# Reordering the drain of a gather-and-project kernel: residuals, put-by sums, the last gathers and the final test

## The chip, the cores and the metric

The kernel runs on one core of one Trainium2 chip. The metric is the device time of one execution in microseconds; the median of several executions counts. The inputs are `x` (4096 x 512), `adj` (4096 x 4096), `W` (512 x 2048, four heads of 512) and `a`, all fp32; the output is 4096 x 512 fp32.

## The reference, cut to what matters

```python
ht  = (h @ W).reshape(N, 4, 512).transpose(1, 0, 2)
src = einsum('hnd,hd->hn', ht, a[:, :512, 0]); dst = einsum('hnd,hd->hn', ht, a[:, 512:, 0])
e   = leaky_relu(src[:, :, None] + dst[:, None, :], 0.01) + adj[None]
att = softmax(e, axis=-1)
x   = layernorm(x + einsum('hij,hjd->hid', att, ht).mean(axis=0))
```

The entries of `adj` reach 1e9, so that in nearly every row one neighbour, the one with the row's largest entry, takes the whole softmax. Then the attention of a row is `x[column of that entry] @ mean over heads of W`. The kernel computes this, and proves it row by row with a bound: the gap between the largest and the second largest entry must exceed a multiple of the largest norm of a row of `x` times the norms of the head vectors. If a row fails, a general path runs behind a branch; with these inputs it does not.

## The kernel before, in words

The 4096 rows stand in 32 blocks of 128 rows (`NB = 32`; a row of a block is a partition). The program is written in the order in which its instructions are to stand; each engine (PE, DVE, ACT, POOL, SP) then runs its own instructions in that order, and one that waits holds back all that stand behind it on its engine.

One pass `t` of the main loop handles a stage of several blocks at once:

- SP loads block `t + 5` of `adj` (2 MB a block, `load_adj`). `hold` holds `x` and later the output rows.
- DVE takes maxima over segments of block `t` (`segment_maxima`, L169), then `find_segment(t)` finds the eight largest (L176) and the best segment's index (L178). POOL turns the index into a row number (L180) and gathers that segment of each row, the "lead" (L186, 128 rows of 128 bytes); it also computes where the segment starts (L191).
- DVE finds the place within the lead of block `t - 2` (`find_column`, L208), POOL adds the segment's start (L210) and gathers the 128 rows of `x` that the columns name (L196, tile `y`, 256 KB).
- PE turns block `t - 3` (`turn`, four transposes, L223), ACT copies the result to SBUF (L225, `yt`), and PE multiplies it by the mean weight in four steps of 128 rows (`products`, L238; a step is two matmuls in the trace[...]), into a PSUM tile `o`. Pool `o` has four buffers of one bank; `tp` has two, `px` and `pv` one each.
- For blocks 0 to 23 PE adds the residual `x` with an identity matmul (`residual`, L231), and ACT takes sums and squares (`stats`, L260 and L262), POOL the reciprocal root (`rstd`, L265 to L267) and ACT writes the normalised row into `hold` (`finish`, L271).

The last eight blocks are special. `BEHIND = 24` and `LATE = 28`. For blocks 24 to 27 ("put by") ACT copies the product out of PSUM to a spare `adj` buffer (`put_by`, L251), because their `x` has not been loaded yet; it is added later (`add_x`, L254). Blocks 28 and 29 get their residual by matmul (L231) in pass 31. Block 30 gets it by a DVE addition (L521), and block 31 is computed in two column halves with residuals of their own (`residual_in_halves`, L276, and `products_of_half`, L280), so that its two halves can be normalised by two engines. Blocks 27 to 31 use DVE statistics (`moments`: L291 and L295 on DVE, a root on ACT, L297; `factor`, L300; `normalise`, L307). Block 31's column is not found through a lead but in the whole row of `adj` (`find_column_in_row`, L216), so that the last gather of `x` need not wait for another gather.

After the loop comes the drain, an order written out by hand. It also holds the proof: `find_inner` (L202) takes the largest entries within the leads of blocks 24 to 31, `bound` (parts 0 to 3) the largest norm of `x` over all rows through two tiny PE operations (L379, L385), `test` six small DVE operations on all blocks (L394 to L400), `count` a tiny matmul (L404) and `report` three small DVE operations (L408 to L411). The stores of the last blocks stand in SP's queue in a fixed order.

In a few lines, the part of the drain around the change before it:

```python
find_column(NB - 2); add_x(nc.gpsimd, BEHIND); add_x(nc.gpsimd, BEHIND + 1)
find_column_in_row(NB - 1); add_x(nc.gpsimd, BEHIND + 2)
products(LATE, KB - 1, KB); residual_in_halves(NB - 1); turn(NB - 3)
```

Of the kernel before, what the change touches and what calls it, by code (L numbers as in the profile page):

```python
# [9 lines left out]
F32 = mybir.dt.float32  # L10
U32 = mybir.dt.uint32
I32 = mybir.dt.int32
AF = mybir.ActivationFunctionType
OP = mybir.AluOpType
# [6 lines left out]
P = 128  # L21
# [47 lines left out]
def leading_rows(ctx, tc, x, adj, W, a, out, ident, v, n_bad, any_bad):  # L69
# [8 lines left out]
    nc = tc.nc  # L78
# [66 lines left out]
    nc.gpsimd.memset(ones, 1.0)  # L145
    width = once.tile([P, 2], U32, name="width")
    nc.gpsimd.iota(width, pattern=[[E_EARLY - E, 2]], base=E, channel_multiplier=0)
    power = once.tile([P, 2], F32, name="power")
    nc.gpsimd.memset(power, -0.5)
    eps = once.tile([P, 1], F32, name="eps")  # L150
    nc.gpsimd.memset(eps, EPS)
# [22 lines left out]
    def find_segment(ib):  # L174
        seg = seg_of.pop(ib)
        nc.vector.max(out=top[:, ib, :], in_=seg)  # L176
        at = small.tile([P, 8], U32, name="at")
        nc.vector.max_index(at, top[:, ib, :], seg)  # L178
        row = small.tile([P, 1], U32, name="row")
        nc.gpsimd.tensor_tensor(row, at[:, 0:1], first[:, ib : ib + 1], op=OP.add)  # L180
        early = ib < EARLY
        if early:
            lead = lead_pool.tile([P, E_EARLY], F32, name="lead_early", bufs=8)
        else:
            lead = lead_pool.tile([P, E], F32, name="lead")
        nc.gpsimd.indirect_dma_start(  # L186
            out=lead, out_offset=None, in_=adj_segs_early if early else adj_segs,
            in_offset=bass.IndirectOffsetOnAxis(ap=row[:, :1], axis=0),
        )
        start = at_of[ib] = small.tile([P, 1], U32, name="start")  # L190
        nc.gpsimd.tensor_tensor(start, at[:, 0:1], width[:, int(early) : int(early) + 1], op=OP.mult)  # L191
        lead_of[ib] = lead

    def gather_rows(ib, col):
        y = y_t[ib] = y_pool.tile([P, D], F32, name="y")
# [5 lines left out]
    def find_inner(ib):  # L201
        nc.vector.max(out=inner[:, ib, :], in_=lead_of[ib])  # L202

    def find_column(ib):
        if ib < BEHIND:
            find_inner(ib)
        within = small.tile([P, 8], U32, name="within")
        nc.vector.max_index(within, top[:, ib, :], lead_of[ib])  # L208
        col = small.tile([P, 1], U32, name="col")
        nc.gpsimd.tensor_tensor(col, at_of.pop(ib), within[:, 0:1], op=OP.add)  # L210
        gather_rows(ib, col)
# [15 lines left out]
    def residual(ib):  # L227
        start = ib not in o_ps
        if start:
            o_ps[ib] = psum.tile([P, D], F32, name="o")  # L230
        nc.tensor.matmul(o_ps[ib], ident, hold[:, ib, :], start=start, stop=False)  # L231

    def products(ib, lo=0, hi=KB):
        start = ib not in o_ps
        if start:
            o_ps[ib] = psum.tile([P, D], F32, name="o")
        for kb in range(lo, hi):
            nc.tensor.matmul(  # L238
                o_ps[ib], yt_of[ib][:, kb, :], w_sum[:, kb, :],
                start=(start and kb == 0), stop=(kb == KB - 1),  # L240
            )

    def row_norm(ib):
        sq = rows.tile([P, D], F32, name="sq")
        nc.scalar.activation(sq, hold[:, ib, :], AF.Square, accum_out=xx[:, ib : ib + 1])  # L245
# [5 lines left out]
        nc.scalar.copy(o_ps["by"][:, ib - BEHIND, :], o_ps.pop(ib))  # L251

    def add_x(engine, ib):
        engine.tensor_add(hold[:, ib, :], hold[:, ib, :], o_ps["by"][:, ib - BEHIND, :])  # L254
        o_ps[ib] = hold[:, ib, :]

    def stats(ib):
        o, i = o_ps[ib], slice(ib, ib + 1)
# [14 lines left out]
    def residual_in_halves(ib):  # L273
        o_ps[ib] = [psum.tile([P, D // 2], F32, name="o") for _ in range(2)]
        for k, o in enumerate(o_ps[ib]):
            nc.tensor.matmul(o, ident, hold[:, ib, ts(k, D // 2)], start=True, stop=False)  # L276
# [45 lines left out]
    def store(queue, lo, n):  # L322
        queue.dma_start(out_rows[:, ds(lo, n), :], hold[:, ds(lo, n), :])
# [49 lines left out]
    def bound(part):  # L373

        if part == 0:
            xm = once.tile([P, 1], F32, name="xm")
            nc.vector.tensor_reduce(xm, xx, axis=AX.X, op=OP.max)
            px = of_bound[0] = psum.tile([1, P], F32, name="px", bufs=1)
            nc.tensor.transpose(px, xm, ident)  # L379
        elif part == 1:  # L380
            nc.vector.tensor_reduce(xg, of_bound[0], axis=AX.X, op=OP.max)
            nc.scalar.activation(xg, xg, AF.Sqrt)
        elif part == 2:
            pb = of_bound[2] = psum.tile([P, 1], F32, name="px", bufs=1)
            nc.tensor.matmul(pb, ones[0:1, :], xg, start=True, stop=True)  # L385
        else:
            nc.vector.tensor_mul(lead_by, of_bound[2], vn)
            nc.vector.tensor_scalar(lead_by, lead_by, 1.05, 110.0, op0=OP.mult, op1=OP.add)
# [29 lines left out]
    for t in range(NB):  # L418
        if t == NB // 2:
            tc.mark_branch_hint_location("general", engines=HINTED)  # L420
        if t in x_at:
            load_x(*x_at[t])
        if t + AHEAD == NB - 1:
            load_x(LATE, Q)
        load_adj(t + AHEAD)
        middle = 1 if t == NB - 1 else 2
        segment_maxima(t, 0, middle)
        if t >= COLUMN:
            find_column(t - COLUMN)
        segment_maxima(t, middle, PIECES)  # L430
        pair = FINISH <= t < BEHIND + FINISH and t % 2 == 0
        if pair:
            rstd(slice(t - FINISH, t - FINISH + 2))
        if t == NB - 1:
            for ib in (BEHIND, BEHIND + 2):
                load_x(ib, 2)
        find_segment(t)
        if t < 2:
            mean_of_heads(t)
        elif t == 2:  # L440
            mean_of_heads(2)
            mean_of_heads(3)
        if t == 0:
            turn_a()
        turned = [(*vectors[0], turn_w(*vectors.pop(0))) for _ in range(vectors_at.get(t, 0))]
        if t == 16:
            head_norms()
        ib = t - PROJECT
        if t == NB - 1:
            for late in range(LATE, NB):  # L450
                row_norm(late)
            residual(LATE)
            residual(LATE + 1)
        if ib >= 0:
            turn(ib)
            if ib > BEHIND:
                products(ib - 1, KB - 1, KB)
            if ib < BEHIND:
                residual(ib)
        for some in turned:  # L460
            head_vector(*some)
        if ib >= 0:
            products(ib, 0, KB if ib < BEHIND else KB - 1)
        if t >= BEHIND + STATS:
            put_by(t - STATS)
        elif t >= STATS:
            stats(t - STATS)
            row_norm(t - STATS)
        if pair:
            finish(t - FINISH)  # L470
            finish(t - FINISH + 1)

    for ib in range(BEHIND, LATE):
        row_norm(ib)
    for ib in range(0, 2 * Q, Q):
        store(nc.sync, ib, Q)
    for ib in range(2 * Q, BEHIND, 2):
        store(nc.sync, ib, 2)
    find_column(NB - 2)
    add_x(nc.gpsimd, BEHIND)  # L480
    add_x(nc.gpsimd, BEHIND + 1)
    find_column_in_row(NB - 1)
    add_x(nc.gpsimd, BEHIND + 2)
    products(LATE, KB - 1, KB)
    residual_in_halves(NB - 1)
    turn(NB - 3)
    products(NB - 3, 0, KB - 1)
    moments(LATE)
    for ib in range(BEHIND, NB):
        find_inner(ib)  # L490
    bound(0)
    products(NB - 3, KB - 1, KB)
    stats(BEHIND)
    factor(LATE)
    normalise(LATE, o_ps.pop(LATE))
    bound(1)
    turn(NB - 2)
    bound(2)
    add_x(nc.vector, LATE - 1)
    stats(BEHIND + 1)  # L500
    moments(LATE - 1)
    products(NB - 2, 0, 2)
    bound(3)
    test()
    pg = count()
    products(NB - 2, 2, KB - 1)
    stats(BEHIND + 2)
    rstd(slice(BEHIND, BEHIND + 2))
    rstd(slice(BEHIND + 2, BEHIND + 3))
    moments(NB - 3)  # L510
    report(pg)
    turn(NB - 1)
    factor(LATE - 1, shift=True)
    factor(NB - 3)
    normalise(NB - 3, o_ps.pop(NB - 3))
    finish(BEHIND)
    finish(BEHIND + 1)
    products(NB - 2, KB - 1, KB)
    products_of_half(NB - 1, 0)
    products_of_half(NB - 1, 1)  # L520
    nc.vector.tensor_add(hold[:, NB - 2, :], o_ps[NB - 2], hold[:, NB - 2, :])  # L521
    o_ps[NB - 2] = hold[:, NB - 2, :]
    moments(NB - 2)
    stats_of_half(NB - 1, 0)
    factor(NB - 2)
    normalise(NB - 2, o_ps.pop(NB - 2))
    finish(BEHIND + 2)
    finish(BEHIND + 3)
    stats_of_half(NB - 1, 1)
    moments(NB - 1)  # L530
    factor(NB - 1, shift=True)
    finish_in_halves(NB - 1)
    for ib, n in ((NB - 4, 1), (NB - 3, 1), (BEHIND, 2), (NB - 2, 1), (BEHIND + 2, 2)):
        store(nc.sync, ib, n)
    store(nc.sync, NB - 1, 1)

# [152 lines left out]
```

## Time and profile before

| What | Value |
|---|---|
| Median of 3 runs | 236.35 us (236.19 to 236.41) |
| The profiled execution's own time | 235.55 us |
| Its span in the profile | 233.9 us |
| Granted clock of PE over the span | 0.965 |
| PE busy | 197.9 us (85%) |
| DVE busy | 192.0 us (82%) |
| ACT busy | 111.8 us (48%) |
| POOL busy | 101.1 us (43%) |
| DMA | 97.06 MB, mean 415 GB/s |
| Last load of `adj` landed, last PE matmul ended | 207.6 us, 228.64 us |

The span runs from the first to the last instruction of the profiled execution; the execution's own time is 1.65 us longer, for what lies around it. Times below are microseconds from the start of the span. The drain proper is the stretch from 207.6 us to the end: the last quarter of `adj` block 31 is in SBUF, and what remains is the search in the last blocks, the last gathers of `x`, the products of blocks 28 to 31, and the normalisation and stores of blocks 24 to 31. The table's shares of busy time are over the whole span and say little about these 26 us; the timeline and the chain of waits do.

### The profile page before, as it was taken

The numbers are of one execution on the slowest core, as the hardware profiler recorded it, in microseconds if no ns is written. First come the engines' busy times: TensorE is split into PE (matmuls) and PEld (weight loads), VectorE is DVE, ScalarE is ACT, GpSimd is POOL, SyncE is SP. The second block draws the span as 40 slices with busy tenths as digits, with TensorE's granted clock in tenths as the row PEclk, the third lists the DMA queues.
The fourth block names the chain that finished last, engine by engine and source line by source line (L and its number), as shares of the span: only waits on it lengthen the run. The fifth ranks groups of instructions, "written<-read, shape, count | busy, mean of one in ns | idle before, by whom it ended". The sixth has DMA issues, their size and how long they took to land.

```text
span 233.9 us, 2499 instructions
## 1 busy us (share of the span) xinstructions
PE 197.9 (85%) x683; PEld 103.0 (44%) x683; DVE 192.0 (82%) x302; ACT 111.8 (48%) x267; POOL 101.1 (43%) x216
## 2 busy tenths in 40 slices
PE   0097959999999899999969968888886989998990
PEld 0034526565656565655424424343433434334460
DVE  1726975689969996999689999998699999979872
ACT  2002012155756547474747464646464285355782
POOL 2022242415526462646343555464364546438330
PEclk9999799999999999999997999999995899999997
DMA  5999999999999999999999999999999999999995
GB/s 226 443 419 424 443 419 432 430 433 413 438 427 417 425 434 434 432 417 426 432 430 436 421 435 423 433 413 433 426 429 418 424 423 425 418 423 416 418 371 220
DMA packets 13697, 97.06 MB, mean 415 GB/s; under 512 B 2152, under 2 KB 2664, under 8 KB 7792
## 3 DMA queue, kind: packets, MB, share of 16 engines
q1 hardware_dynamic: 10080, 88.08, 89.1%
q0 software_dynamic: 3584, 8.77, 9.5%
q8 instruction: 6, 0.10, 0.2%
q14 instruction: 11, 0.09, 0.1%
q10 hardware_dynamic: 16, 0.02, 0.0%
HBM read 88.47 MB, written 8.39 MB: 414 GB/s over the span
## 4 chain that ended last, share of the span: by engine, by line
DMA 49%; PE 14%; issue 12%; POOL 12%; DVE 10%; ACT 2%; POOLq 0%; SPq 0%; DVEq 0%
DMA adj_t<-in_adj_dram 42%; PE o L238 9%; DVE seg L169 8%; DMA y<-in_x_dram,col 7%; POOL lead L186 3%; POOL y L196 3%; PE tp L223 2%; PE o L280 2%; POOL sd L266 1%; PE o L231 1%; POOL lead_early L186 1%; POOL start L191 1%; POOL row L180 1%; POOL col L210 1%; ACT yt L225 1%
## 5 line engine op out<-in xcount | busy, mean ns | idle before, releaser
L169 DVE TENSOR_REDUCE seg<-adj_t 128x128 f32<-128x2048 f32 (+3 forms) x68 | 145.9, 2148 | 28.9 <-DMA adj_t<-in_adj_dram 28.7
L238 PE MATMUL o<-w_sum,yt 128*128 128x512 f32 x248 | 116.2, 610 | 1.7 <-ACT yt L225 1.7
L238 PEld LDWEIGHTS o<-w_sum,yt 128*128 128x128 f32 x248 | 45.1, 194 | 56.0 <-issue 43.5
L225 ACT COPY yt<-tp 128x512 f32<-128x512 f32 x32 | 18.8, 588 | 44.3 <-PE tp L223 44.3
L196 POOL DMA_INDIRECT y<-in_x_dram,col x32 | 30.8, 962 | 15.9 <-POOL col L210 15.1
L328 PE MATMUL o<-hold,ident 128*128 128x512 f32 x32 | 18.8, 743 | 15.3 <-POOL row L180 11.3
L223 PE MATMUL tp<-ident,y 128*128 128x128 f32 x128 | 20.5, 284 | 10.5 <-DMA y<-in_x_dram,col 10.4
L231 PE MATMUL o<-hold,ident 128*128 128x512 f32 x52 | 28.3, 631 | 0.3 <-DMA hold<-in_x_dram 0.3
L180 POOL TENSOR_TENSOR row<-at,first 128x1 uint32<-128x1 uint32 x32 | 6.0, 188 | 46.5 <-DVE at L178 46.3
L223 PEld LDWEIGHTS tp<-ident,y 128*128 128x128 f32 x128 | 15.5, 147 | 23.0 <-issue 21.7
L346 ACT COPY wt<-tp 128x512 f32<-128x512 f32 x16 | 9.2, 587 | 32.0 <-PE tp L344 32.0
L186 POOL DMA_INDIRECT lead_early<-in_adj_dram,row x18 | 18.2, 1010 | 8.9 <-POOL row L180 8.9
L210 POOL TENSOR_TENSOR col<-start,within 128x1 uint32<-128x1 uint32 x31 | 5.8, 188 | 35.5 <-DVE within L208 35.5
L245 ACT ACTIVATE sq<-hold 128x512 f32<-128x512 f32 x32 | 19.8, 619 | 0.0
L352 PEld LDWEIGHTS pv<-at_d,wt 128*128 128x128 f32 x128 | 16.3, 191 | 6.8 <-ACT wt L346 3.5
L328 PEld LDWEIGHTS o<-hold,ident 128*128 128x128 f32 x32 | 7.3, 238 | 24.5 <-POOL row L180 11.3
L329 ACT ACTIVATE w_sum<-o 128x512 f32<-128x512 f32 x4 | 2.4, 598 | 31.5 <-PE o L328 31.5
L271 ACT ACTIVATE hold<-o,nm,sd 128x512 f32<-128x512 f32 x24 | 17.2, 770 | 0.0
L186 POOL DMA_INDIRECT lead<-in_adj_dram,row x14 | 14.1, 1005 | 7.1 <-POOL row L180 7.1
L262 ACT ACTIVATE sq<-o,nm 128x512 f32<-128x512 f32 x24 | 16.5, 688 | 0.8
L352 PE MATMUL pv<-at_d,wt 128*128 128x2 f32 x128 | 15.3, 244 | 0.6 <-ACT wt L346 0.6
L260 ACT ACTIVATE sq<-o 128x512 f32<-128x512 f32 x24 | 14.6, 608 | 0.0
(90 smaller groups left out, 152.5 us busy)
## 6 DMA issues: line engine op xcount, KB each, us to landing
adj_t<-in_adj_dram SPq DMA_DIRECT2D x27, 2048.0 KB, 31.4
hold<-in_x_dram SPq DMA_DIRECT2D x7, 1024.0 KB, 32.1
adj_t<-in_adj_dram SPq DMA_DIRECT2D x6, 1024.0 KB, 28.1
out_dram<-hold SPq DMA_DIRECT2D x10, 512.0 KB, 14.1
adj_t<-in_adj_dram SPq DMA_DIRECT2D x8, 512.0 KB, 6.3
hold<-in_L_gnn_W_dram SPq DMA_DIRECT2D x4, 1024.0 KB, 17.3
out_dram<-hold SPq DMA_DIRECT2D x2, 1024.0 KB, 14.0
hold<-in_x_dram SPq DMA_DIRECT2D x2, 512.0 KB, 14.8
```

Of the source, the lines that this page charges most:

```text
L169: nc.vector.tensor_reduce(seg_of[ib][:, ts(k, N // e // n)], adj_t[ib][:, ts(k, N // n)].rearrange("p (s e) -> p s e", e=e), axis=AX.X, op ...
L186: nc.gpsimd.indirect_dma_start(out=lead, out_offset=None, in_=adj_segs_early if early else adj_segs, in_offset=bass.IndirectOffsetOnAxis(a ...
L196: nc.gpsimd.indirect_dma_start(out=y, out_offset=None, in_=x, in_offset=bass.IndirectOffsetOnAxis(ap=col[:, :1], axis=0),)
L223: nc.tensor.transpose(tp[:, kb, :], y[:, ts(kb, P)], ident)
L225: nc.scalar.copy(yt, tp)
L231: nc.tensor.matmul(o_ps[ib], ident, hold[:, ib, :], start=start, stop=False)
L238: nc.tensor.matmul(o_ps[ib], yt_of[ib][:, kb, :], w_sum[:, kb, :], start=(start and kb == 0), stop=(kb == KB - 1),)
L245: nc.scalar.activation(sq, hold[:, ib, :], AF.Square, accum_out=xx[:, ib : ib + 1])
L262: nc.scalar.activation(sq, o, AF.Square, bias=nm[:, i], accum_out=sd[:, i])
L271: nc.scalar.activation(hold[:, ib, :], o_ps.pop(ib), AF.Identity, bias=nm[:, i], scale=sd[:, i])
L328: nc.tensor.matmul(o, ident, hold[:, w_at + kb * H + h, :], start=(h == 0), stop=(h == H - 1))
L352: nc.tensor.matmul(pv[:, kb, h : 2 * H : H], wt[:, k, :], at_d[:, k, h : 2 * H : H], start=(k == 0), stop=(k == KB - 1),)
```

## The change

- The residual matmuls of blocks 28 and 29 move from pass 31 (in front of 28's turn) to pass 30 (in front of 27's turn).
- `residual_in_halves(31)` moves behind `turn(29)`.
- `find_segment` is split: the POOL part becomes `fetch_segment`. For block 31 it is called only in the drain, behind 30's gather of `x`, and its segment start, which nobody reads, is not computed.
- `add_x` writes the sum into the put-by tile instead of into `hold`, and the order of POOL's additions changes: 24's stands in front of 30's column and gather, 25's behind the lead of block 31, 26's behind 31's gather. 27's stays on DVE and moves behind `moments(29)`.
- The root of the largest norm is no longer taken of one number in the middle of `bound`, but of all 32 norms per partition at once on ACT, behind the last `row_norm`.
- `bound`, the inner maxima of blocks 24 to 30 and the statistics of 24 and 25 on ACT move ahead; `find_inner(31)` stands alone behind `moments(28)`; `test` follows, and only then `factor(28)` and `normalise(28)`.
- Block 30's products stand in front of `turn(31)` in full, with `count` behind their first step. Before, the last step stood behind `turn(31)`.
- One `rstd` for three blocks replaces two; the `finish` calls and the order of the last stores move.

```diff
     def find_segment(ib):
...
-        at = small.tile([P, 8], U32, name="at")
+        at = at_of[ib] = small.tile([P, 8], U32, name="at")
         nc.vector.max_index(at, top[:, ib, :], seg)
+        if ib < NB - 1:
+            fetch_segment(ib)
+
+    def fetch_segment(ib):
+        at = at_of.pop(ib)
         row = small.tile([P, 1], U32, name="row")
...
     def add_x(engine, ib):
-        engine.tensor_add(hold[:, ib, :], hold[:, ib, :], o_ps["by"][:, ib - BEHIND, :])
-        o_ps[ib] = hold[:, ib, :]
+        o = o_ps[ib] = o_ps["by"][:, ib - BEHIND, :]
+        engine.tensor_add(o, o, hold[:, ib, :])
...
             nc.vector.tensor_reduce(xg, of_bound[0], axis=AX.X, op=OP.max)
-            nc.scalar.activation(xg, xg, AF.Sqrt)
...
         if t == NB - 1:
             for late in range(LATE, NB):
                 row_norm(late)
+        if t == NB - 2:
             residual(LATE)
             residual(LATE + 1)
...
     for ib in range(BEHIND, LATE):
         row_norm(ib)
+    nc.scalar.activation(xx, xx, AF.Sqrt)
...
+    add_x(nc.gpsimd, BEHIND)
     find_column(NB - 2)
-    add_x(nc.gpsimd, BEHIND)
+    fetch_segment(NB - 1)
     add_x(nc.gpsimd, BEHIND + 1)
     find_column_in_row(NB - 1)
     add_x(nc.gpsimd, BEHIND + 2)
     products(LATE, KB - 1, KB)
+    turn(NB - 3)
     residual_in_halves(NB - 1)
-    turn(NB - 3)
-    products(NB - 3, 0, KB - 1)
+    products(NB - 3, 0, 1)
+    bound(0)
+    for ib in range(BEHIND, NB - 1):
+        find_inner(ib)
+    bound(1)
+    products(NB - 3, 1, KB - 1)
+    bound(2)
+    stats(BEHIND)
+    stats(BEHIND + 1)
     moments(LATE)
-    for ib in range(BEHIND, NB):
-        find_inner(ib)
-    bound(0)
+    find_inner(NB - 1)
+    bound(3)
+    test()
+    turn(NB - 2)
+    stats(BEHIND + 2)
+    rstd(slice(BEHIND, BEHIND + 3))
     products(NB - 3, KB - 1, KB)
-    stats(BEHIND)
     factor(LATE)
     normalise(LATE, o_ps.pop(LATE))
-    bound(1)
-    turn(NB - 2)
-    bound(2)
+    products(NB - 2, 0, 1)
+    pg = count()
+    products(NB - 2, 1, KB)
+    report(pg)
+    moments(NB - 3)
     add_x(nc.vector, LATE - 1)
-    stats(BEHIND + 1)
-    moments(LATE - 1)
-    products(NB - 2, 0, 2)
-    bound(3)
-    test()
-    pg = count()
-    products(NB - 2, 2, KB - 1)
-    stats(BEHIND + 2)
-    rstd(slice(BEHIND, BEHIND + 2))
-    rstd(slice(BEHIND + 2, BEHIND + 3))
-    moments(NB - 3)
-    report(pg)
-    turn(NB - 1)
-    factor(LATE - 1, shift=True)
     factor(NB - 3)
     normalise(NB - 3, o_ps.pop(NB - 3))
     finish(BEHIND)
+    turn(NB - 1)
     finish(BEHIND + 1)
-    products(NB - 2, KB - 1, KB)
+    moments(LATE - 1)
+    finish(BEHIND + 2)
     products_of_half(NB - 1, 0)
     products_of_half(NB - 1, 1)
     nc.vector.tensor_add(hold[:, NB - 2, :], o_ps[NB - 2], hold[:, NB - 2, :])
     o_ps[NB - 2] = hold[:, NB - 2, :]
+    factor(LATE - 1, shift=True)
+    finish(LATE - 1)
     moments(NB - 2)
     stats_of_half(NB - 1, 0)
     factor(NB - 2)
     normalise(NB - 2, o_ps.pop(NB - 2))
-    finish(BEHIND + 2)
-    finish(BEHIND + 3)
     stats_of_half(NB - 1, 1)
...
-    for ib, n in ((NB - 4, 1), (NB - 3, 1), (BEHIND, 2), (NB - 2, 1), (BEHIND + 2, 2)):
+    for ib, n in ((NB - 4, 1), (NB - 3, 1), (BEHIND, 2), (BEHIND + 2, 2), (NB - 2, 1)):
```

More of the change, by code (lines that the diff above doesn't have):

```diff
@@ L147, in leading_rows @@
     nc.gpsimd.iota(width, pattern=[[E_EARLY - E, 2]], base=E, channel_multiplier=0)
-    power = once.tile([P, 2], F32, name="power")
+    power = once.tile([P, 3], F32, name="power")
     nc.gpsimd.memset(power, -0.5)
@@ L189, in find_segment @@
         )
-        start = at_of[ib] = small.tile([P, 1], U32, name="start")
-        nc.gpsimd.tensor_tensor(start, at[:, 0:1], width[:, int(early) : int(early) + 1], op=OP.mult)
         lead_of[ib] = lead
+        if ib < NB - 1:
+            start = at_of[ib] = small.tile([P, 1], U32, name="start")
+            nc.gpsimd.tensor_tensor(start, at[:, 0:1], width[:, int(early) : int(early) + 1], op=OP.mult)
     def gather_rows(ib, col):
```

## The prediction

> **What bounds the kernel now.** I read the 40 slices first: the DMA row stays at 9 up to the last slice, so nothing can be won before the last load lands at 207.6 us, and no edit touches the bytes. The change lives in the drain, so I read the chain of waits there (columns: start, length, what).
>
> ```profile
> 201.30 7.26 DMA y<-in_x_dram,col
> 208.56 0.14 issue
> 208.70 0.63 PE tp L223 x4
> 209.33 4.37 PE o L238 x10
> 213.70 0.86 PE o L276 x4
> 214.56 0.45 PE tp L223 x4
> 215.02 0.02 issue
> 215.04 0.59 ACT yt L225
> 215.63 0.04 issue
> 215.68 2.84 PE o L238 x6
> ...
> 220.60 1.98 PE o L238 x4
> 222.59 0.15 PE px L404 x2
> 222.74 1.05 PE o L238 x2
> 223.79 0.44 PE tp L223 x4
> 224.23 0.86 PE o L238 x2
> 225.09 3.55 PE o L280 x16
> ```
>
> From 28's turn to 228.64 the chain is PE's own queue, broken only by two waits for ACT's copy of `yt` (0.65 us each, at 215.0 and 219.9). A step of `products` is two matmuls, 0.86 us. Next, who feeds PE: the timeline of POOL (start, length, line, what it writes and reads; in brackets the idle time before it and what ended it).
>
> ```profile
> 209.72 0.19 POOL L180 TENSOR_TENSOR row<-at,first 128x1 uint32<-128x1 uint32 x1 [2.91 <-DVE at L178]
> 210.42 0.96 POOL L186 DMA_INDIRECT lead<-in_adj_dram,row  x1 [0.51 <-POOL row L180]
> 212.01 0.97 POOL L196 DMA_INDIRECT y<-in_x_dram,col  x1 [0.27 <-POOL col L210]
> 213.00 2.50 POOL L254 TENSOR_TENSOR hold<-hold,adj_t 128x512 f32<-128x512 f32 x2
> 216.25 0.96 POOL L196 DMA_INDIRECT y<-in_x_dram,col  x1 [0.76 <-issue]
> ```
>
> And of DVE:
>
> ```profile
> 211.07 4.42 DVE L216 FIND_INDEX8 col<-top,adj_t 128x8 uint32<-128x4096 f32 x1
> 216.22 0.81 DVE L202 MAX8 inner<-lead 128x8 f32<-128x32 f32 x8
> 217.22 0.81 DVE L307 TENSOR_SCALAR hold<-o,mv,sd 128x512 f32<-128x512 f32 x1
> ```
>
> The landings, asked tile by tile: 31's lead 5.4 us after 210.42 (215.8), 30's `y` 6.5 after 212.01 (218.5), 31's `y` 7.0 after 216.25 (223.2). So 31's turn at 223.79 stands only about 0.5 us behind its data: even a perfect PE order gains no more than that and a little. The lead of 31 is used at 216.9 without a wait, and 28 leaves its PSUM buffer at 218.03, 2.6 us before 30's first product (220.60) wants one.
>
> **What the Trainium skill says.** "DMA: Bandwidth & Descriptors", sections "SWDGE vs HWDGE vs iDMA" and "Two DMAs through the same engine are not ordered": one software queue is allocated for POOL's DMAs, and within a queue of an engine descriptors start in order. The trace agrees: each lead landed 0.6 to 2.9 us after the `y` issued before it, never ahead. "PSUM — Partial Sum Buffer", "The four PSUM rules" and the specifications: eight banks, a matmul's output in one. This kernel uses all eight (o 4, tp 2, px, pv): no spare for block 30. "GPSIMD Engine Reference", "Engine selection": a two-input elementwise operation is about twice as slow there as on VectorE; here 1.27 against 0.67 us (L254 on both).
>
> **The change, part by part.**
>
> *Residuals of 28 and 29 one pass earlier.* Four matmuls, 1.88 us, go from 206.5 to about 201.95, in front of 27's turn (202.48 before, after a 0.55 us wait for `y`). Their `x` landed at 201.44 (176.43 + 25.0), so no wait by 0.5 us. 27's turn and copy go back by some 1.3 us, but 27's three products then end near 207.8 and 28's turn waits for its `y` until 208.56 anyhow. ACT has its idle 2.3 us before 28's copy to take the delay. Cost 0, hidden by 28's gather; if it lost that cover, at most 1.3 us. PE is at 213.70 as before.
>
> *31's residuals behind 29's turn.* The turn ends at 214.15, the residuals run to 215.0 beside ACT's copy (to 214.8). The wait of 0.65 us is gone. 29's first product starts at 215.0, not 215.68.
>
> *POOL.* 24's addition (1.25 us) stands in front of 30's column. It waits for `x` of 24, landed 208.64 (193.13 + 15.5), so it runs 208.7 to 210.0, in POOL's idle stretch; the place in 30's lead is known at 210.99. Cost 0 with 1 us of slack. 31's row number, lead and start leave the space ahead of 30's column. Column at 211.06, then 0.19 and the 0.54 us that POOL takes to a gather after an idle stretch (seen at 200.76 to 201.30): 30's `y` issues at 211.8 instead of 212.01, landing 218.3. Then 31's row number at 212.8 and its lead at **213.3 instead of 210.42**. 25's addition then ends at about 215.5, when DVE's search ends (215.49): 31's `y` issues at 216.25 as now, lands 223.2; a quarter of a microsecond either way costs nothing, as will be seen.
>
> *31's lead.* With the median 5.4 us of the last leads (5.0 to 6.4) it lands at 218.7; behind 30's `y` by the least 0.6 seen, at 218.9. I take 218.8, and 218.3 to 219.6 as the ends.
>
> *DVE, the new order.* After 215.49: norm maximum, seven inner maxima (0.1 each), `xg`, moments of 28 (0.83); done near 217.6. Then `find_inner(31)` **waits for 31's lead until 218.8**. Behind it in DVE's queue stand `test`, 28's reciprocal and 28's `normalise`. From landing: 0.1 to wake (210.64 to 210.74 for lead 30), 0.1, then 1.19 from L387 to the end of `test` (220.41 to 221.60), 0.99 for L300 and L307 (217.04 to 218.03), 0.05 for PE to wake: 2.43 us. So 28 frees its PSUM buffer at 221.23.
>
> *PE.* 29's products and the two tiny operations of `bound` end near 217.9; 30's turn waits for `y` (218.3) and ends near 219.0; 29's last step covers the copy and ends at 219.85. 30's first step needs a buffer: 29 and 31's halves hold three, 28 the fourth. The built program's order shows the same: that matmul has gained a wait for DVE. So PE **stands from 219.85 to 221.23**. From there: four steps 3.44, `count` 0.15, turn of 31 0.45 (its `y` is 2 us early), the copy 0.65, which no product covers any more since 30's last step moved in front of the turn, and the halves 3.55: 8.24 us, end 229.47. Before: 228.64. **+0.83.**
>
> *DVE behind it.* `report` waits for `count` behind 30's first step: 221.23 + 0.86 + 0.26 = 222.35. Then `report` 0.38, moments of 29 0.83, 27's addition 0.71, 29's factor and normalise 1.06, moments of 27 0.83, 30's addition 0.73, 27's factor 0.38, moments of 30 0.83, first half 0.45, 30's factor and normalise 0.76: 6.96, end 229.3, with 0.2 for two waits for ACT's roots 229.5. So DVE reaches the second half as late as PE does, and little slip is left: I take +0.9. The 2.0 us from the second half to the last activation and the last store (2.3 us) keep their length.
>
> *At nothing:* the root over 32 norms (0.2 us for the one number; under 0.4 for this) runs behind the last `row_norm`, at 213.3, when ACT is idle to 214.2; it takes 0.2 us of ACT and a hop out of `bound`, which is not what test waits for. Statistics of 24 and 25 on ACT run 214.8 to 217.6, in front of 30's copy at 219.0. One `rstd` for three (0.7 to 0.9) starts when 26's statistics end near 221 and is done before ACT wants it at 224. The sums in their own tile have the same shapes. SP's stores: 28's goes from 218.06 to 221.3 and holds nothing, as 29's behind it is later; 26/27 now ahead of 30, both before 31. The DMA share was 0.49 at 228 to 229, so there is room.
>
> **Sum.** Span 233.9 + 0.9 = 234.8, own time 235.55 + 0.9 = 236.45. The profiled execution is 0.80 below the median, so I put the shift on the median: 236.35 + 0.9 = **237.25 us**. The lead's ends give +0.4 to +1.7: 236.75 to 238.05.
>
> **Rivals.**
> - *31's lead comes early* (ends on the other side). If it lands before 218.0, normalise of 28 ends by 220.4 and PE loses nothing (228.64 - 8.24 = 220.40). At 217.3 or earlier the gather of 31's `y` sets the end: 223.2 + 0.14 + 0.45 + 0.65 + 3.55 = 228.0, 0.65 less: 235.7. For it: the bubble at 215 does go. Against: it would need 4.7 us from issue to break even and 4.0 for all of it; no lead took under 5.0. Chance 0.09.
> - *The drain hides it* (no change): the store queue or the tail's slack absorbs the shift, or the lead lands near 218.2: 236.35 +- 0.4. Against: DMA share 0.49 at 228; PE's chain runs straight to the end. 0.11.
> - *24's addition blocks POOL.* If `x` of 24 lands after 209.7 instead of 208.64, POOL holds 30's gather and 31's lead one for one; 1 us late gives 238.2. A load of that queue took 25.0 us a little earlier, but that was twice the size. 0.1.
> - The forecast itself: 0.70.
>
> **The numbers.** 0.2% (0.47 us) is about what a measurement of this kernel can tell. Slower takes the forecast and the third rival: 0.80; same 0.11; faster 0.09. The range 236.4 to 238.4 takes in the ends of the forecast, the upper half of "no change" and the third rival up to 1.2 us late, and leaves out the first rival.
>
> **What would show it.** Right: `inner` of 31 waiting for DMA lead by about 1.2 us; a PE wait of about 1.4 us ahead of 30's first L244 put down to DVE `hold` (L313); one wait for `yt` of 0.65 ahead of the halves; none at 29's copy; last L286 near 229.5. Wrong: 31's lead issued before 212.5 or landed before 218, no DVE wait in front of 30's products, or 31's turn waiting for its `y`.

## The result and the profile after

The kernel after the change takes **237.16 us** (median of 8 runs, 236.77 to 237.67), the kernel before beside it 236.21 us (8 runs, 235.91 to 236.41). The medians differ by 0.95 us. The ratio is **1.0043**, 95% interval 1.0031 to 1.0056: slower, by more than the noise. (A ratio here is estimated from all executions of the two kernels beside each other and need not be the quotient of the two medians.) The profiled execution of after took 237.13 us with a span of 235.6 us.

The chain of waits of the kernel after, from the search on (start, length, what):

```profile
213.07 5.27 DMA lead<-in_adj_dram,row
...
218.37 0.20 DVE inner L208
...
219.88 0.82 DVE hold L313
...
220.84 1.10 PE o L244 x2
...
225.33 0.59 ACT yt L231
...
225.97 3.73 PE o L286 x16
```

Before, this stretch of the chain was PE's own queue. Now it leaves PE: it runs through the gather of 31's lead, nine small DVE operations of `find_inner(31)` and `test`, and 28's reciprocal and normalisation (L313), and only then comes back to block 30's first product. The timeline of PE in the kernel after shows the same from the other side (in brackets: idle time before, and what ended it):

```profile
215.05 1.10 PE L244 MATMUL o<-w_sum,yt 128*128 128x512 f32 x2
...
220.84 1.10 PE L244 MATMUL o<-w_sum,yt 128*128 128x512 f32 x2 [1.10 <-DVE hold L313]
...
225.97 3.72 PE L286 MATMUL o<-w_sum,yt 128*128 128x256 f32 x16 [0.68 <-ACT yt L231]
```

The first line is the wait that the change removes: 29's first product starts without one. The second is the new wait for the PSUM buffer, the third the copy of 31 that nothing covers. What led to the second stands in the timelines of POOL and DVE of the kernel after:

```profile
209.26 1.27 POOL L261 TENSOR_TENSOR adj_t<-adj_t,hold 128x512 f32<-128x512 f32 x1 [1.74 <-DMA hold<-in_x_dram]
...
211.62 0.97 POOL L202 DMA_INDIRECT y<-in_x_dram,col  x1 [0.60 <-POOL col L216]
...
213.07 0.96 POOL L191 DMA_INDIRECT lead<-in_adj_dram,row  x1 [0.27 <-POOL row L185]
```

```profile
218.37 0.20 DVE L208 MAX8 inner<-lead 128x8 f32<-128x32 f32 x1 [0.97 <-DMA lead<-in_adj_dram,row]
218.48 0.14 DVE L392 TENSOR_TENSOR lead_by<-px,vn 128x1 f32<-128x1 f32 x1
```

24's addition, 30's gather and then 31's lead, in this order; DVE stands 0.97 us for the lead. One thing to keep for later: the second matmul of `bound` (L390), whose result the next DVE line (L392) reads, ran on PE from 217.91 to 218.29, and the lead landed at 218.34. The wait bears the name of the one that came last.

**The account.** Two points serve as marks in every kernel: the issue of 27's gather of `x` (POOL timeline, 196.11 before, 196.49 after), which lies ahead of all edits, and the start of the search in block 31's row (DVE, `FIND_INDEX8`). The stretches from one to the next, in us; from PE's end to the issue of the last store it is 2.05 to 2.07 everywhere.

| Kernel | 27's gather to search | search to PE's end | last store, issue to landing | ratio to before (95%) |
|---|---|---|---|---|
| before | 14.96 | 17.55 | 2.27 | 1 |
| after | 14.33 | 18.87 | 2.88 | 1.0043 (1.0031 to 1.0056) |
| e1 28 normalised at once | 14.23 | 17.52 | 3.43 | 0.9992 (0.9973 to 1.0012) |
| e2 30 in another bank | 14.24 | 17.60 | 3.38 | 1.0004 (0.9987 to 1.0021) |
| e3 lead early | 14.37 | 19.26 | 3.19 | 1.0078 (1.0050 to 1.0105) |
| e4 copy covered | 14.32 | 18.08 | 2.97 | 1.0011 (0.9995 to 1.0027) |
| e5 e1 and e4 | 14.13 | 17.13 | 3.92 | 1.0004 (0.9992 to 1.0016) |
| e6 e5, old store order | 14.20 | 16.96 | 4.21 | 0.9999 (0.9985 to 1.0012) |
| e7 lead early, 24 behind | 14.24 | 18.76 | 2.83 | 1.0044 (1.0029 to 1.0059) |
| e8 before, 28 behind the test | 14.81 | 19.97 | 2.58 | 1.0138 (1.0105 to 1.0171) |
| e9 before, halves behind | 14.90 | 17.58 | 2.66 | 0.9988 (0.9976 to 0.9999) |
| e10 before, residuals early | 14.34 | 17.43 | 3.13 | **0.9974** (0.9961 to 0.9987) |
| e11 e5, 1 MB fewer stores | 14.13 | 17.05 | 3.32 | 0.9955 (0.9937 to 0.9973) |
| e12 before, 1 MB fewer stores | 14.82 | 18.01 | 2.33 | 0.9997 (0.9982 to 1.0012) |

So after loses 1.32 us between search and PE's end and 0.61 us on the last store, and wins 0.63 us ahead of the search: +1.30 us. With the 0.38 us by which the profiled execution of after issued 27's gather later, that is the difference of the spans, 1.68 us; the medians differ by 0.95 us. The stretches come from one execution each, so tenths of a microsecond in them count for little and the ratios for more.

### The profile page after: what moved, and what is told of

The parts are those of the page before. It is cut to its first block, busy times and chain, and to the rows that moved or that the text cites. A ratio compares the mean times of both kernels' runs of the same rounds, so it can differ in the third digit from the quotient of the medians.

```text
span 235.6 us, 2495 instructions
## 1 busy us (share of the span) xinstructions
PE 193.8 (82%) x683; PEld 99.8 (42%) x683; DVE 192.0 (82%) x302; ACT 111.7 (47%) x267; POOL 100.7 (43%) x212
## 4 chain that ended last, share of the span: by engine, by line
DMA 46%; POOL 18%; issue 17%; DVE 12%; PE 3%; ACT 1%; POOLq 0%; SPq 0%; DVEq 0%
DMA adj_t<-in_adj_dram 42%; DVE seg L169 8%; POOL y L202 6%; POOL lead L191 5%; DMA lead<-in_adj_dram,row 5%; POOL sd L272 2%; PE o L244 2%; PE o L286 2%; POOL row L185 1%; POOL start L198 1%; POOL col L216 1%; DVE col L222 1%; POOL lead_early L191 1%; DVE at L178 1%; DVE top L176 1%
## 5 line engine op out<-in xcount | busy, mean ns | idle before, releaser
L244 PE MATMUL o<-w_sum,yt 128*128 128x512 f32 x248 | 114.7, 603 | 1.8 <-DVE hold L313 1.1
L244 PEld LDWEIGHTS o<-w_sum,yt 128*128 128x128 f32 x248 | 44.1, 190 | 54.9 <-issue 41.5
L334 PE MATMUL o<-hold,ident 128*128 128x512 f32 x32 | 18.1, 719 | 16.5 <-DMA hold<-in_L_gnn_W_dram 16.5
L229 PE MATMUL tp<-ident,y 128*128 128x128 f32 x128 | 19.7, 276 | 13.4 <-DMA y<-in_x_dram,col 13.3
L237 PE MATMUL o<-hold,ident 128*128 128x512 f32 x52 | 26.7, 597 | 0.2 <-DMA hold<-in_x_dram 0.2
L229 PEld LDWEIGHTS tp<-ident,y 128*128 128x128 f32 x128 | 14.3, 141 | 26.7 <-issue 26.2
```

The costliest lines, as they stand in the source:

```text
L229: nc.tensor.transpose(tp[:, kb, :], y[:, ts(kb, P)], ident)
L244: nc.tensor.matmul(o_ps[ib], yt_of[ib][:, kb, :], w_sum[:, kb, :], start=(start and kb == 0), stop=(kb == KB - 1),)
L334: nc.tensor.matmul(o, ident, hold[:, w_at + kb * H + h, :], start=(h == 0), stop=(h == H - 1))
```

## Experiments

The theory: 28 is normalised behind `test`, so its PSUM buffer comes free late and PE stands in front of 30's first product; the copy of 31 adds a wait of its own. The rivals: DVE as a whole is late, whichever buffer waits; the lead's late issue is the cause, not the place of the normalisation; the additions on POOL; the stores. Unless said otherwise the edit is made to the kernel after.

### e1: normalise 28 behind its own moments

```diff
     moments(LATE)
+    factor(LATE)
+    normalise(LATE, o_ps.pop(LATE))
     find_inner(NB - 1)
...
-    factor(LATE)
-    normalise(LATE, o_ps.pop(LATE))
```

> The changed kernel with one move: 28's reciprocal and normalise stand right behind 28's moments on DVE, ahead of 31's inner maxima and of the test. Theory 1 (28's PSUM buffer is held behind a test that waits for 31's lead): 30's first product loses its wait for DVE, starts near 219.7 instead of 220.84, 31's turn is then set by its y (near 223.1) or by 30's last product, the last half ends near 228.1 instead of 229.70; time 1.2 to 1.6 us below the changed kernel's 237.16, about 235.7, which is also under the kernel before. Theory 2 (the loss is the copy of 31's transposes that no product covers, 0.65 us, and a later last store): the stall goes but the copy stays uncovered, gain at most 0.3 us, 236.9 or more.

Measured: 236.00 us (before beside it 235.96), ratio 0.9992 (0.9973 to 1.0012). In the timeline of PE in e1, 29's last step and 30's first are now one group of four without a gap:

```profile
217.93 1.96 PE L244 MATMUL o<-w_sum,yt 128*128 128x512 f32 x4
```

DVE used the lead at 218.26 without waiting: the lead was as late as in after (issued at 212.38, landed at 217.74), but by then nobody who waits for a buffer stood behind it. Moving two calls brings back the whole loss; the uncovered copy of 31 and a longer last store (3.43 us) are still there.

### e2: block 30 in another bank, DVE left as it is

```diff
-            o_ps[ib] = psum.tile([P, D], F32, name="o")
+            if ib == NB - 2:
+                o_ps[ib] = psum.tile([P, KB, P], F32, name="tp", bufs=2).rearrange("p k c -> p (k c)")
+            else:
+                o_ps[ib] = psum.tile([P, D], F32, name="o")
```

> The changed kernel, but block 30's product is written into a tp buffer instead of an o buffer, so it needs none that 28 holds; DVE's order is untouched, 28's normalise still stands behind the test. Theory 1: the wait ahead of 30's first product goes (start near 219.7), count follows at 220.6 without a wait (the test ends near 219.8), the last half ends near 228.2; 235.7 to 236.0. Theory 2: 236.9 or more. If DVE's lateness itself (not the buffer) were the cause, the end would also stay near 237.1 although PE no longer waits.

Measured: 236.25 us, ratio 1.0004 (0.9987 to 1.0021). The timeline of PE and that of DVE in e2:

```profile
219.82 1.10 PE L247 MATMUL tp<-w_sum,yt 128*128 128x512 f32 x2
```

```profile
220.26 0.81 DVE L316 TENSOR_SCALAR hold<-o,mv,sd 128x512 f32<-128x512 f32 x1
```

DVE is as late as in after (it waited 1.10 us for the lead, and normalised 28 at 220.26), yet 30's product has begun 0.44 us before that, and PE does not wait ahead of it. So it is the buffer and not DVE's lateness. The Trainium skill ("PSUM — Partial Sum Buffer", "The four PSUM rules") has a matmul's output in one bank of 512 fp32 columns; a buffer of `tp` is such a bank, and the trace agrees: 30's first step ran there in 1.10 us, as in the kernel after.

### e3: 31's lead issued early, as in the kernel before

```diff
-        if ib < NB - 1:
-            fetch_segment(ib)
+        fetch_segment(ib)
...
-    fetch_segment(NB - 1)
     add_x(nc.gpsimd, BEHIND + 1)
```

> The changed kernel, but 31's lead is fetched in the loop as in the kernel before, ahead of 30's column. Theory 1: the lead lands near 215.8, 31's inner maxima wait for nothing, the test ends about 1 us sooner, 28 is normalised by about 219.8 and 30's products start near 219.9; 30's y issues 0.2 us later; the end is 0.9 to 1.3 us sooner, about 236.0. Theory 2: no gain, 237.0 to 237.3.

Measured: 237.60 us, ratio 1.0078 (1.0050 to 1.0105), where a gain was expected: no faster than after (1.0043), rather slower. The timelines of POOL and of PE in e3 tell why:

```profile
211.28 1.28 POOL L260 TENSOR_TENSOR adj_t<-adj_t,hold 128x512 f32<-128x512 f32 x1
212.51 0.19 POOL L215 TENSOR_TENSOR col<-start,within 128x1 uint32<-128x1 uint32 x1
212.97 0.97 POOL L201 DMA_INDIRECT y<-in_x_dram,col  x1 [0.27 <-POOL col L215]
```

```profile
219.52 0.63 PE L228 MATMUL tp<-ident,y 128*128 128x128 f32 x4 [1.72 <-DMA y<-in_x_dram,col]
```

With the lead back in front, 24's addition stands behind it, not in POOL's idle stretch: 30's gather went out 2.5 us after the search began instead of 0.8, and 30's turn waited 1.72 us. That is what the third rival of the prediction feared, 24's addition in the way of 30's gather, but here the order causes it and not a late `x`; in the change itself it does not happen. The experiment moved two things, and says little about the lead.

### e7: the lead early, and 24's addition behind 30's gather

```diff
+        fetch_segment(ib)
...
-    add_x(nc.gpsimd, BEHIND)
     find_column(NB - 2)
-    fetch_segment(NB - 1)
+    add_x(nc.gpsimd, BEHIND)
```

> The changed kernel with 31's lead fetched in the loop as before, and 24's addition on POOL put back behind 30's gather, so that 30's y is not held up as it was in the run with the lead alone. Theory 1 as predicted (31's lead sets when 28's buffer comes free): the last half ends 0.9 to 1.2 us sooner, 236.0 to 236.3. Theory 1 mended (28's normalise stands behind the test, and the test would wait for the bound's second tiny matmul nearly as long as for the lead: in the run with the lead alone it did so until 7.5 us after the start of the search, where the lead had landed at 7.6): only 0.1 to 0.4 us sooner, 236.8 to 237.1.

Measured: 236.84 us, ratio 1.0044 (1.0029 to 1.0059), the same as after. The lead landed at 215.98, before DVE wanted it; counted from the start of the search that is 5.45 us, where it was 7.52 in after. From the timelines of DVE and of PE in e7:

```profile
217.05 0.16 DVE L207 MAX8 inner<-lead 128x8 f32<-128x32 f32 x1
218.06 0.16 DVE L391 TENSOR_TENSOR lead_by<-px,vn 128x1 f32<-128x1 f32 x1 [0.85 <-PE px L389]
```

```profile
220.43 1.10 PE L243 MATMUL o<-w_sum,yt 128*128 128x512 f32 x2 [0.41 <-ACT sq L265]
```

The inner maxima of 31 wait for nothing any more, and `test` stands 0.85 us for the second tiny matmul of `bound`, which PE runs behind 29's third step. 28 is normalised 8.94 us after the search's start, against 9.06 in after. So the lateness of the lead is worth about a tenth of a microsecond, because another wait lies right behind it. (The name of the second wait is doubtful: L265 is a statistic on ACT, as in e4 below; 28's normalisation ended at 220.28, 0.15 us before the matmul.)

### e8: the kernel before, with 28 normalised behind the test

```diff
     moments(LATE)
...
-    factor(LATE)
-    normalise(LATE, o_ps.pop(LATE))
...
     test()
+    factor(LATE)
+    normalise(LATE, o_ps.pop(LATE))
```

> The kernel before with one move: 28's reciprocal and normalise stand behind the test on DVE, as in the change. 31's lead comes early here and nothing else is moved. Theory 1: the buffer for block 30 comes free at about 222.6 instead of 218.0, 30's first product starts some 2 us later than 220.6, and the time is 1.5 to 2.0 us longer, 237.7 to 238.2. If the late buffer were not the cause, no more than 0.3 us longer.

Measured: 238.77 us, ratio 1.0138 (1.0105 to 1.0171). From the timeline of PE in e8:

```profile
223.02 1.96 PE L238 MATMUL o<-w_sum,yt 128*128 128x512 f32 x4 [2.52 <-DVE hold L307]
```

This is the loss put into a kernel that has nothing else of the change: early lead, old additions, old products. It is larger than expected (2.8 us, not 1.5 to 2.0), since in this order 27's addition (0.67 us), 27's moments and a wait of 1.85 us for `bound`'s first operation stand ahead of `test` as well. With e1 it shows the place of the normalisation as cause from both sides.

### e4: 30's last step behind 31's turn

```diff
-    products(NB - 2, 1, KB)
+    products(NB - 2, 1, KB - 1)
...
     moments(LATE - 1)
     finish(BEHIND + 2)
+    products(NB - 2, KB - 1, KB)
     products_of_half(NB - 1, 0)
```

> The changed kernel, but 30's last step stands behind 31's turn, as before the change, so that it covers ACT's copy of 31's transposes; the wait for 28's buffer stays. Both theories: the 0.65 us wait ahead of the halves goes. Theory 1: the last half ends 0.5 to 0.65 sooner, 236.5 to 236.7, still over the kernel before. Theory 2: all of the loss but the store's, 236.2 to 236.5.

Measured: 236.31 us, ratio 1.0011 (0.9995 to 1.0027). In the timeline of PE in e4 the wait for the buffer stays and that for the copy is gone:

```profile
220.20 1.10 PE L244 MATMUL o<-w_sum,yt 128*128 128x512 f32 x2 [1.27 <-ACT sq L268]
...
224.50 3.70 PE L286 MATMUL o<-w_sum,yt 128*128 128x256 f32 x16
```

PE's end comes 0.79 us nearer to the search, and the ratio falls by 0.0032, some 0.75 us. Together with e1 (1.35 us to PE's end, 0.0051) that is more than the whole loss. If the two simply added up, the kernel would be faster than before; e5 tests this.

### e5 and e6: both, and then the old order of the stores

e5 has the diffs of e1 and e4. e6 adds

```diff
-    for ib, n in ((NB - 4, 1), (NB - 3, 1), (BEHIND, 2), (BEHIND + 2, 2), (NB - 2, 1)):
+    for ib, n in ((NB - 4, 1), (NB - 3, 1), (BEHIND, 2), (NB - 2, 1), (BEHIND + 2, 2)):
```

> The changed kernel with both moves of the runs before: 28's normalise ahead of 31's inner maxima and the test, and 30's last step behind 31's turn. If the two losses on PE are separate, the last half ends about 0.65 us sooner than with the first move alone, some 0.6 us sooner against the search of row block 31 than in the kernel before, and the time is 235.3 to 235.7 where the kernel before has 236.2. If the stores of the last blocks now set the end (in the run with the first move alone the DMA engines were full until 229 and the last store took 3.4 us instead of 2.3), the gain on PE is not seen in the time: 235.8 to 236.2.

> The same as the run beside it (both moves), with the last stores in the order of the kernel before (30's ahead of 26's and 27's). If the new order of stores makes the last store late, the last store takes 2.3 to 2.6 us instead of about 3.2 and the time is 0.4 to 0.8 us shorter than the run beside it. If it is the amount of stores still under way, not their order, there is no difference (within 0.2 us).

Measured: e5 236.09 us, ratio 1.0004 (0.9992 to 1.0016); e6 235.83 us, ratio 0.9999 (0.9985 to 1.0012). PE's end comes 0.4 to 0.6 us nearer to the search than in the kernel before, and the time does not. The stores of the last 13 us in e5, in the view of their tile `out_dram`:

```profile
DMA to landing us min/median/max: 3.9/5.4/5.7
```

In before the same view has 2.3/3.5/4.0. The mean DMA share was 1.02 in 222 to 227 us and 0.96 in 227 to 230 us (before: 0.94 and 0.83). The last store took 3.9 and 4.2 us where it took 2.27 before. The order of the stores makes no difference that can be seen: the intervals of e5 and e6 overlap almost wholly.

### e9 and e10: two parts of the change alone, in the kernel before

e9 moves `residual_in_halves(NB - 1)` behind `turn(NB - 3)`; e10 gives the residuals of 28 and 29 the line `if t == NB - 2:`. Nothing else is changed.

> The kernel before with one edit: 31's residuals stand behind 29's turn. Theory 1 (the edit takes away a PE wait of 0.65 us, but the end of PE is held 0.5 us further on by 31's y): no PE wait for yt ahead of 29's first product, PE ends 0.3 to 0.6 us sooner after the search than before's 17.55 us, and the last store takes longer in part for it; 235.8 to 236.1 us against 236.2. Rival (all of PE's time here is slack): PE's end where it was within 0.1 us, 236.2 us.

> The kernel before with one edit: the residuals of 28 and 29 stand one pass earlier, in front of 27's turn. Theory 1 (the wait for 28's y at 208.56 hides them either way): 28's turn starts within 0.1 us of its y, PE's end after the search within 0.15 us of 17.55, 236.2 us within 0.3. Rival (the delay of 27's products and copies reaches the drain): 28's turn late by 0.3 to 1.3 us, 236.5 to 237.5 us.

Measured: e9 235.62 us, ratio 0.9988 (0.9976 to 0.9999); e10 235.60 us, ratio **0.9974** (0.9961 to 0.9987), before beside both 236.12 us. From the timeline of PE in e9:

```profile
215.38 2.82 PE L238 MATMUL o<-w_sum,yt 128*128 128x512 f32 x6
...
223.72 0.63 PE L223 MATMUL tp<-ident,y 128*128 128x128 f32 x4 [0.25 <-DMA y<-in_x_dram,col]
```

The wait at 29's copy is gone and 31's turn now waits for its data. Measured from 28's turn, PE's end is 0.42 us nearer (19.50 us, before 19.92), as expected; measured from the search it is not (17.58, before 17.55), because 28's turn came 0.45 us later against the search (28's `y` took 7.51 us in this execution, before 7.26). The time is a little below the 235.8 to 236.1 us expected. From the timeline of PE, first in before, then in e10:

```profile
202.48 0.63 PE L223 MATMUL tp<-ident,y 128*128 128x128 f32 x4 [0.55 <-DMA y<-in_x_dram,col]
...
208.70 0.63 PE L223 MATMUL tp<-ident,y 128*128 128x128 f32 x4 [0.30 <-DMA y<-in_x_dram,col]
```

```profile
203.71 0.63 PE L223 MATMUL tp<-ident,y 128*128 128x128 f32 x4
...
207.75 0.60 PE L223 MATMUL tp<-ident,y 128*128 128x128 f32 x4
```

These are the turns of 27 and 28; in before both wait for their `y`, in e10 neither does. PE reaches 28's turn 0.95 us sooner, and the search starts 0.62 us sooner after 27's gather (14.34 us, before 14.96). The expected 236.2 us (within 0.3) was missed on the good side, and the rival with it. Of the versions that write the whole output, e10 is the one that beats both kernels clearly; the interval of e9 ends just under 1. Whether it is the residuals as such that bring this gain is doubtful: see the last section.

### e11 and e12: fewer stores

Both leave out the stores of blocks 20 to 23 (`range(2 * Q, BEHIND - 4, 2)`), e11 in e5, e12 in the kernel before; their output is incomplete, and only their times are of use.

> e5 (28 normalised behind its moments, 30's last step behind 31's turn) with the stores of blocks 20 to 23 left out (1 MB of 8; those output rows are not written). Theory 1 (in e5 the backlog of stores takes what PE gained): the last store takes 2.2 to 2.6 us instead of 3.9, PE ends about 17.1 us after the search's start or sooner, 234.3 to 235.0 us, and at least 0.5 us below e12. Rival (the last store is long for a reason of its own, not the backlog): it takes 3.5 us or more again, 235.8 to 236.2 us.

> The kernel before with the stores of blocks 20 to 23 left out (those output rows are not written), as the measure for e11. Theory 1 (before is bound by PE's queue, its last store takes 2.27 us with no backlog): the last store takes 2.1 to 2.4 us, PE's end moves by at most 0.4 us (the gathers may land sooner), 235.5 to 236.3 us. Rival (the store backlog sets before's time too): 234.5 to 235.3 us, as e11.

Measured: e11 235.30 us, ratio 0.9955 (0.9937 to 0.9973); e12 235.92 us, ratio 0.9997 (0.9982 to 1.0012). The stores of the last 13 us in e11, in the same view as those of e5:

```profile
DMA to landing us min/median/max: 3.3/3.6/4.2
```

1 MB less to store gives the kernel before nothing that can be told from noise and e5 about 0.5% (1.0004 to 0.9955): e5 was held back by its stores at least in part, before is not. (PE's end in e12, 18.01 us after the search, is late because 28's turn came late against it, with a `y` of 7.44 us; from 28's turn it is 19.92 us, as before.) But the last store fell only to 3.3 us, not to the expected 2.2 to 2.6, with a DMA share of 0.56 in 227 to 230 us, and the time to 235.3 and not 234.3 to 235.0. Part of its length is therefore not the backlog of those blocks; the last section says what the trace shows beside it.

## Why the prediction was right

The shift was forecast as +0.9 us, and the medians differ by 0.95 us. That they agree within 0.05 us is luck, as the terms below show. The mechanism stood: 28's buffer held behind `test`, the uncovered copy of 31. e1, e2, e4 and e8 show each of them by intervention. Step by step:

- **31's residuals behind 29's turn**: the wait went as forecast, and e9 puts its worth by itself at about 0.1%, with an interval that ends just under 1.
- **POOL**: 30's `y` at 211.62 (forecast 211.8), 31's lead at 213.07 (213.3). 24's addition began at 209.26, not 208.7, so it ended 0.3 us before 30's column, not 1 us: nearer to the third rival than the prediction thought.
- **The lead** landed at 218.34, 0.46 us before the value taken and at the early end of its range. From there to 28's buffer it took 2.36 us (forecast 2.43), and PE waited 1.10 us (1.38).
- **The sum from 30's first product to PE's end was too short**: 8.86 us, not 8.24. The first step took 1.10 us behind its wait and the three behind `count` 2.77, where 0.86 and 2.58 were reckoned; the halves took 3.73 us behind their wait, not 3.55. The prediction priced all of them by matmuls that overlap the one ahead, though the chain of before that it shows has other cases too: 1.98 us for two steps behind a wait, 1.05 for the one step behind `count`. This error of +0.62 and the early landing of the lead offset each other in part; PE's end came at 229.70 (forecast 229.47).
- **DVE as late as PE**: not so. At the second half DVE waited 0.55 us for PE; the 0.07 us added for it had no ground.
- **"The last store keeps its length"** failed: 2.88 us against 2.27. In e5 part of the added length is stores still under way: without 1 MB of them (e11) it falls from 3.92 to 3.32 us. In after itself it is not that; see the last section. The Trainium skill ("DMA: Bandwidth & Descriptors", "Anatomy of one DMA — SWDGE (gpsimd) path") fits a DMA as 2.0 us plus its bytes at 436 GB/s; by that fit 256 KB would take an estimated 2.6 us. These stores are issued by SP and took 2.27 to 4.21 us, so no constant fits them.
- **The residuals of 28 and 29 "cost 0, hidden by 28's gather"** failed on the other side: alone they gain 0.26% (e10), and in all kernels that have the edit the way to the search is shorter, by about 0.6 us. The forecast took 28's gather and 30's lead to land when they landed before.
- **"A hop out of `bound`, which is not what test waits for"** was wrong: e7 shows that `test` waits for it as soon as the lead is early. The first rival (lead early, 235.7 us) had its price wrong for this reason: with the lead 2.1 us sooner against the search, e7 takes 236.84 us. The lead was the last of two waits by 0.05 us, and the prediction saw only the one.
- **"No spare for block 30"** in PSUM was too strong: in e2 a buffer of `tp` holds 30's product, and PE does not wait for it.

So the total is right while its terms are off, by the account above: 0.63 us won ahead of the search that was not seen, against 0.5 us more between search and PE's end (1.32, forecast 0.83) and 0.6 us more on the last store. For the two profiled executions that makes +1.30 us; the medians differ by less, since the profiled execution of before lies 0.66 us below the median of the 8 runs of before, and that of after 0.03 us below its own.

## What to carry to other kernels

When a reader of a PSUM buffer moves down in an engine's order, ask at once who wants that buffer next and what all the instructions now ahead of the reader wait for: the wait that the profile names is only the last of them, and removing it may move nothing (e7). Price a group of matmuls that will start behind a wait from a row that did so too. And when PE's end comes forward, the next limit may lie in the last stores: look at how long each takes to land before you promise the gain.

## What was not expected of the hardware

Two gathers of 256 KB one after the other shared their latency in one of two ways, with the same issue distance (5.2 to 5.3 us). In the four profiled kernels with the residuals of 28 and 29 in pass 31 (before, e8, e9, e12), 27's `y` took 6.0 to 6.2 us, 28's 7.3 to 7.5 and 30's lead 6.1 to 6.4. In the nine with the residuals in pass 30 for which the landings are on record (e1 to e7, e10, e11), it was 7.2 to 7.6, 6.0 to 6.3 and 5.4 to 5.7. The later kind is the better: 27's longer gather is covered by the residuals, and 28's turn and the search come sooner.

The records of single DMA packets in the traces show what goes with it. The profile's page lists a queue `q8 instruction` with 6 transfers. The fifth, of 16 KB, begins 5.0 to 5.6 us after the issue of 27's gather in the ten kernels with the residuals in pass 30, and 9.9 to 10.1 us after it in the four others. In before it runs from 206.21 to 207.16 us, when 28's gather is about to land and 30's lead is under way; two of the gather's 4 KB packets end at 207.59 and 207.96, the others by 206.88. In e10 it runs from 201.33 to 202.30, when 27's gather is about to land and 30's lead is not yet issued; one 4 KB packet of that gather ends at 202.73, the others by 201.66. So the longer gather is each time the one that is about to land when this transfer comes, and the edit may gain by moving the transfer rather than by the residuals as such. No run moves the one without the other, and the records do not say on which DMA engine a packet ran: this is a fit of times in fourteen traces, not a test.

The last store of 256 KB took from 2.27 us (before) to 4.21 us (e6), though nothing in it was changed. Two things go with its length. One is earlier stores: the last packet of a 512 KB store begins 0.85 us after the issue of the last store in before, but 1.35 us after it in e5 and 2.28 us in e6. In after and in e7 there is less of this than in before (0.45 us after the issue, and none), and yet the last store took 2.88 and 2.83 us. There the other thing shows, 8 KB transfers of the queue `q14 instruction`. In e7 two of them end 1.72 and 1.75 us after the issue, and the last 16 of the store's 2 KB packets follow in two rows of eight, from 1.72 and 1.74 us; in after one ends at 1.67 us, and the last row of eight begins at 1.66 us. In before these transfers begin only at 1.78 us, when every 2 KB packet of the store has begun (by 1.57 us). So the 0.6 us that after adds on the last store fit a transfer of instructions ahead of some of the store's packets. This too is read from times alone, and no run changed it.
